# A two-layer graph attention kernel: the planner's lock is taken from the weights' dot products, and its leads are replaced

## The chip, the core and the metric

The kernel runs on one core of a Trainium2 chip. A core has five engines that run their own queues of instructions in order: TensorE (PE in the profile, with its weight loads as PEld), VectorE (DVE), ScalarE (ACT), GpSimd (POOL) and SyncE (SP, which here only issues DMAs). The metric is the device time of one execution in microseconds. The kernel before takes 3507.43 us, the median of three runs (3507.41 to 3511.81).

## The reference

For each of 32 graphs with 512 nodes and 512 features (fp32) and a 0/1 adjacency matrix, two residual layers are computed. Each normalises its input, applies a relu and adds a graph attention:

```
h = relu(layernorm(x));  x = x + GAT0(h, adj)      # one head, no weights matrix
h = relu(layernorm(x));  x = x + GAT1(adj, h)      # 4 heads of 256, elu, then 1 head of 512

GAT0: s_src = h @ w_src;  s_dst = h @ w_dst
      attn = softmax(mask(leaky_relu(s_src[i] + s_dst[j] + b)))   ;  out = attn @ h
GAT1: xl = h @ W1 (512 x 1024), per head asrc = <xl, a_src>, adst = <xl, a_dst>
      softmax(mask(leaky_relu(asrc[s] + adst[d]))) over s ;  out = attn^T @ xl + b1 ; elu
      the same again with W2 (1024 x 512), one head
```

`asrc` and `adst` are linear in `h`: `asrc = h @ (W1 a_src)`. The kernel uses this. It computes the dot products of the weights' rows with the attention vectors once, on VectorE, and stores them as two extra columns beside each block of weights, so that the projection itself yields the scores.

## The kernel before

**Tiles.** A graph's rows stand in 4 tiles of 128 nodes. x has two places in SBUF, the masks (`m`) five, large results (`big`: edge weights E, features, projections) nine, and PSUM eight banks (`acc`).

**Stages of a graph.** `load_x` (LX); `layer0_scores` (S0): statistics on ACT for graphs 0 and 1 (lines 686 and 691), the power -1/2 on POOL (711), the scaled features on ACT (723), two dots per tile on DVE for the scores (`dot`, line 508, called at 1024 to 1030), an add on POOL (1032), the adjacency's mask on DVE (988, 993) and its transposed copy by SP (958). Then the guard, an upper bound of each row's scores: a row of scores is spread over the partitions by TensorE (`spread`, 676), DVE takes masked maxima (838), POOL adds (845), DVE joins (856). `edge_weights`: per tile a subtraction on POOL (882), a maximum and add on DVE (887), an exponential on ACT (894). `layer0_out` (O0) multiplies E with the features on TensorE (906) and adds into x (924). `layer1_in` (I1): layernorm again, the features turned by copies on ACT (743, 759) and transposing DMAs of SP (750), then `x + b2` on POOL (1074) and a spill of x to DRAM (1082). `layer1_project` (P1) and `layer2_project` (P2) multiply with the weights by a seven-product scheme (Strassen's in Winograd's form; TensorE at 1216), for which POOL forms the sums S1 to S4 of the input's quarters (1098) and the weights have the combinations T1, T2, T3 and -T4. The heads follow (H0 to H3), then `layer2_out` (O2).

**Constants.** Once, at the start, `load_constants` fetches the weights; `scores_1` makes 32 dots over W1's rows (4 row blocks, 4 heads, source and target; 256 elements each), `scores_2` 32 dots over W2's rows and 8 small adds (605); `column_sums` sums W2's columns on TensorE (622) and corrects b2 (637); `sums` forms T1, T2, T3 and -T4 of each matrix, values and score columns apart, on DVE or POOL (657, 658). The score columns of a combination need all the dots of their matrix. P1's second product, S1 times T1, needs T1 with its columns.

**The planner.** The kernel first records all operations with their engines, costs, reads and writes, then `Plan.draft` writes each engine's order by list scheduling: at every step the engine that can start soonest takes its best ready operation, the one with the smallest rank. The rank is the TensorE work recorded ahead of it less 1000 times its lead (`run`), so a larger lead goes first. A lead's name is stage, engine and the number of the operation's kind in that stage: `first S0g:DVE2` is the guard's line 838 of graph 0, `first Clater:DVE3` the dots of W1, `first Clater:DVE4` the weights' sums, `first Clater:DVE5` and `DVE6` the dots of W2, `first Clater:PE8` the column sums, `second S0:DVE7` the feature dots of graph 1. The stages "first", "second" and "last" have leads of their own; the graphs between share theirs.

Operations with `lock=True` on DVE and on POOL exclude each other in the plan:

```
bufs, locks = ops[i][4], ops[i][6]
if locks and e in lock and lock["POOL" if e == "DVE" else "DVE"] > at:
    heapq.heappush(later[e], (lock["POOL" if e == "DVE" else "DVE"], rank[i], i))
    continue
```

If both engines can start at the same instant, the one that stands first in `("PE", "ACT", "DVE", "POOL", "SP")` is served. The lock lives in the plan alone. On the chip only the queues' order and the data's semaphores hold. The tile `junk`, into which all dots, guards and ACT's statistics write values that nobody reads, isn't in the planner's lists either, but the chip's semaphores do order its writers.

Of the kernel before, what the change touches and what calls it, by code (L numbers as in the profile page):

```python
# [43 lines left out]
class Plan:  # L44
# [8 lines left out]
        "first LXsoon:SP0": 67.5, "first Csoon:SP0": 22.3, "first C:SP0": 15.3, "first Csoon:DVE1": -520.9,  # L53
        "first Clater:DVE0": -150.2, "first Clater:SP1": 22.3, "first Clater:DVE2": -516.8, "first S0:ACT0": -617.3,
        "first S0:ACT1": -146.3, "first S0:DVE2": 659.4, "first S0:POOL3": 88.2, "first S0:POOL4": 350.9,
        "first S0:POOL5": -561.2, "first S0:ACT6": 1450.6, "first S0:DVE7": 1411.7, "first S0:POOL8": 870.8,
        "first S0M0:POOL0": 546.3, "first S0M0:DVE1": 311.3, "first S0M0:DVE2": 215.9, "first S0M0:SP3": -1427.8,
        "first S0g:POOL0": -1064.9, "first S0g:PE1": 1717.7, "first S0g:DVE2": 2207.5, "first S0g:POOL3": 846.3,
        "first S0g:DVE4": 3270.6, "first S0e:PE0": -477.2, "first S0e:ACT1": 639.1, "first S0e:POOL2": 1171.2,
        "first S0e:DVE3": 2003.2, "first S0e:ACT4": -114, "first Clater:DVE3": -15523.5, "first Clater:DVE4": -6168.4,  # L60
        "first O0:PE0": -531.4, "first O0:DVE1": -1568.2, "first O0:DVE2": -1088.3, "first Clater:DVE5": -144,
        "first Clater:DVE6": -139.3, "first Clater:DVE7": -897.5, "first Clater:PE8": -49490.4,
        "first Clater:DVE9": -882, "first Clater:DVE10": -993.2, "first Clater:DVE11": -2114.6,
        "first I1:ACT0": -1609.1, "first I1:ACT1": -981.7, "first I1:DVE2": 2894.1, "first I1:POOL3": 3384.7,
        "first I1:POOL4": 3602.7, "first I1:ACT5": -3080.8, "first I1:ACT6": -1207.6, "first I1:SP7": 2767.8,
        "first I1:ACT8": 845.2, "first I1:POOL9": -46.6, "first I1:SP10": -39.2, "second LX:SP0": 301.3,
        "second S0:ACT0": -634.4, "second S0:ACT1": -693.1, "second S0:DVE2": 700.7, "second S0:POOL3": 276.3,
        "second S0:POOL4": 1432.6, "second S0:POOL5": 675.4, "second S0:ACT6": 939.6, "second S0:DVE7": -886.2,
        "second S0:POOL8": 373.7, "second S0M0:POOL0": -592, "second S0M0:DVE1": 8.3, "second S0M0:DVE2": -1244.9,
        "second S0M0:SP3": -919, "second S0g:POOL0": 121.2, "second S0g:PE1": 813.7, "second S0g:DVE2": -737.4,  # L70
        "second S0g:POOL3": 325.2, "second S0g:DVE4": 922.4, "second S0e:PE0": -189.2, "second S0e:ACT1": 1520.1,
        "second S0e:POOL2": 943.7, "second S0e:DVE3": -3018.4, "second S0e:ACT4": -5889.6, "M1:POOL0": -333.9,
        "M1:DVE1": -1310.6, "M1:DVE2": -589.2, "M1:SP3": -1290.8, "P1:POOL0": -315.8, "P1:POOL1": 534, "P1:PE2": -554,
        "P1:ACT3": -366.6, "P1:DVE4": -307.5, "S10:ACT0": -625.6, "S10:PE1": -313.7, "S10:SP2": -162.3,
# [311 lines left out]
def kernel(  # L386
# [187 lines left out]
    def scores_1(att):  # L574
        for k in range(KD):
            for h in range(H):
                q, kk = QUARTER[k // (KD // 2)][h % 2], k % (KD // 2)
                for i in range(2):
                    op(
                        "DVE", on_dve(F + 125),  # L580
                        lambda w=w1_s[q][:, kk, h // 2, :], i=i, h=h: dot(
                            w[:, 2:], flat(att[0])[:, i * HF + h * F : i * HF + (h + 1) * F], w[:, i : i + 1]
                        ),
                        W["w1"]((q, kk)) + att[0](i), W["w1"]((q, kk, h // 2, i)), LATER, lock=True,
                    )

    @plan.part("C")
# [869 lines left out]
```

## Time and profile before

| | us |
|---|---|
| median of three runs | 3507.43 |
| profiled execution, device time | 3510.15 |
| its span, first to last instruction | 3508.4 |
| TensorE busy | 3408.4 |
| TensorE idle from 0 to its first instruction (26.55) | 26.5 |
| TensorE idle from 26 to 122 | 42.8 |
| TensorE idle from 122 to 300 | 13.4 |
| TensorE idle from 400 to 3300 | 8.5 |
| DVE busy from 26 to 122 | 82.4 |
| 64 dots of the weights, one (median) | 0.43 |

Times in the lines of the profile count from the start of the span. In a timeline's line stand the start, the duration, the engine, the line of the kernel, the operation, what it writes and reads, and in brackets the idle time of its engine just before, with what released it. An L508 is one dot; the read of its accumulator (0.08) that overlaps its end is a record of its own, so that dots follow each other every 0.47 us. The 512-element L508 with `ws_r` or `wd_r` are the features' dots of S0; those over `w`, `w_T` and `big` are the weights'.

### The profile page before, as it was taken

To read this page: it belongs to the slowest core of one execution; us is meant where nothing else is said; L and a number is where in the kernel's file an instruction comes from. 1 tells how busy PE (TensorE), PEld (TensorE's weight loads), DVE (VectorE), ACT (ScalarE), POOL (GpSimd) and SP (SyncE) were. 2 spreads that over 40 slices of the span, in tenths; PEclk is the share of its full clock that TensorE was granted. 3 is DMA by queue.
4 is the path that set the end of the run, shared out by engine and by line. 5 is a ranking of instruction groups with operands and counts; after the bars stand their busy time and mean duration, and the time that the engine had idled before them with its cause. 6 is when DMAs were issued, how large, how long until landed. Compare 5 with 4: busy or idle time off the path is not lost.

```text
span 3508.4 us, 49234 instructions
## 1 busy us (share of the span) xinstructions
PE 3408.4 (97%) x15678; PEld 2929.5 (83%) x15678; DVE 2640.2 (75%) x7294; ACT 2067.7 (59%) x3288; POOL 1756.7 (50%) x1929
## 2 busy tenths in 40 slices
PE   4799999999999999999999999999999999999999
PEld 3677888888888888888888888888888888888888
DVE  6875877777877777777777777777777777787674
ACT  3674665556665555665555665555755565755563
POOL 2454455554455554555454555454555454555442
PEclk8899999999999999999999999999999999999999
DMA  5444655555655555655555655555655555655632
GB/s 147 117 124 95 138 147 134 136 143 114 141 138 137 138 140 110 151 137 137 140 133 114 155 136 136 139 136 112 157 134 136 140 134 114 150 136 136 145 88 76
DMA packets 732125, 462.14 MB, mean 132 GB/s; under 512 B 553596, under 2 KB 592728, under 8 KB 731864
## 3 DMA queue, kind: packets, MB, share of 16 engines
q1 hardware_dynamic: 698072, 425.42, 47.6%
q0 software_dynamic: 33792, 33.56, 6.7%
q8 instruction: 124, 2.03, 0.2%
q14 instruction: 137, 1.12, 0.1%
HBM read 289.93 MB, written 68.27 MB: 102 GB/s over the span
## 4 chain that ended last, share of the span: by engine, by line
PE 93%; DVE 3%; DMA 2%; ACT 1%; issue 1%; POOL 1%; DVEq 0%; SPq 0%; POOLq 0%; ACTq 0%
PE acc L906 50%; PE acc L1216 42%; PE acc L790 1%; DVE junk L508 1%; DVE guard L856 1%; DMA big<-row 1%; DVE junk L838 1%; DMA m<-m 0%; DMA v<-row 0%; ACT big L894 0%; DVE big L887 0%; ACT junk L691 0%; ACT junk L686 0%; ACT big L759 0%; POOL big L882 0%
## 5 line engine op out<-in xcount | busy, mean ns | idle before, releaser
L906 PE MATMUL acc<-big,big 128*128 128x257 f32 (+1 forms) x8192 | 1942.4, 381 | 18.8 <-ACT big L894 14.6
L906 PEld LDWEIGHTS acc<-big,big 128*128 128x128 f32 x8192 | 1539.9, 190 | 270.4 <-ACT big L894 22.2
L882 POOL TENSOR_TENSOR big<-m,big 128x512 f32<-128x512 bf16 x768 | 883.6, 1169 | 265.6 <-DMA big<-lines 214.5
L894 ACT ACTIVATE big<-big,ac 128x512 f32<-128x512 f32 x768 | 545.7, 720 | 190.5 <-DVE big L887 187.1
L887 DVE SCALAR_TENSOR_TENSOR big<-acc,ac,big 128x512 f32<-128x512 f32 x768 | 566.9, 743 | 92.9 <-POOL big L882 85.3
L838 DVE CUSTOM_DVE_ANT_0 junk<-m,acc 128x512 bf16<-128x512 bf16 x768 | 520.8, 678 | 53.3 <-ACT acc L817 38.2
L1216 PE MATMUL acc<-w_T,sum 128*128 128x258 f32 (+1 forms) x2048 | 506.8, 381 | 17.3 <-POOL big L490 15.2
L1216 PE MATMUL acc<-w,big 128*128 128x258 f32 (+1 forms) x2048 | 517.4, 381 | 3.8 <-ACT big L759 3.5
L731 ACT COPY big<-acc 128x258 f32<-128x258 f32 (+1 forms) x376 | 139.9, 374 | 561.1 <-PE acc L1216 556.8
L1216 PEld LDWEIGHTS acc<-w_T,sum 128*128 128x128 f32 x2048 | 387.2, 190 | 73.9 <-POOL big L490 15.6
L1216 PEld LDWEIGHTS acc<-w,big 128*128 128x128 f32 x2048 | 386.3, 190 | 64.6 <-ACT big L759 4.3
L732 DVE COPY big<-acc 128x258 f32<-128x258 f32 (+1 forms) x392 | 166.1, 424 | 326.0 <-PE acc L1216 323.2
L1227 DVE TENSOR_TENSOR big<-acc,big 128x258 f32<-128x258 f32 (+1 forms) x576 | 241.2, 420 | 117.8 <-PE acc L1216 116.0
L1299 ACT ACTIVATE v<-acc,minus_one 128x256 f32<-128x256 f32 x512 | 228.4, 470 | 147.6 <-DVE acc L1292 83.7
L759 ACT COPY big<-v 128x1024 uint16<-128x1024 uint16 x256 | 295.9, 1157 | 22.0 <-DMA v<-row 21.8
L743 ACT COPY row<-v 128x1024 uint16<-128x1024 uint16 x256 | 265.7, 1040 | 13.1 <-DMA v<-row 10.9
L924 DVE SCALAR_TENSOR_TENSOR x<-acc,r,x 128x256 f32<-128x256 f32 x512 | 240.0, 480 | 39.1 <-PE acc L906 31.8
L1216 PE MATMUL acc<-w,sum 128*128 128x258 f32 (+1 forms) x1024 | 254.8, 382 | 0.0
L1216 PE MATMUL acc<-w_-T,big 128*128 128x258 f32 (+1 forms) x1024 | 252.8, 380 | 0.0
L845 POOL TENSOR_TENSOR guard<-ac,guard 128x4 f32<-128x4 f32 (+1 forms) x128 | 26.1, 204 | 444.2 <-DVE guard L838 427.0
L1292 DVE SCALAR_TENSOR_TENSOR acc<-acc,r,b_r 128x256 f32<-128x256 f32 x512 | 238.9, 485 | 2.9
L1303 DVE SCALAR_TENSOR_TENSOR v<-v,acc 128x256 f32<-128x256 f32 x512 | 204.8, 411 | 47.0 <-ACT v L1299 43.8
(89 smaller groups left out, 3412.2 us busy)
## 6 DMA issues: line engine op xcount, KB each, us to landing
big<-lines SPq DMA_DIRECT2D x378, 256.0 KB
row<-lines SPq DMA_DIRECT2D x189, 256.0 KB
x<-in_x_dram SPq DMA_DIRECT2D x32, 1024.0 KB
m<-in_adj_dram POOLq DMA_DIRECT2D x64, 512.0 KB, 5.8
spill<-x SPq DMA_DIRECT2D x32, 1024.0 KB
x<-spill SPq DMA_DIRECT2D x32, 1024.0 KB
out_dram<-x SPq DMA_DIRECT2D x30, 1024.0 KB
v<-row SPq DMA_TRANSPOSE x256
```

Source lines behind the costliest of these rows:

```text
L743: lambda: nc.scalar.copy(e.at.bitcast(U16).rearrange("p (b f) -> p b f", b=2), values_of().bitcast(U16).rearrange("p (f b) -> p b f", b=2)),
L759: nc.scalar.copy(out.bitcast(U16).rearrange("p k t (n b) -> p k t n b", b=2), values_of().bitcast(U16).rearrange("p (b t k n) -> p k t n b ...
L838: lambda t=t, j=j, a_row=a_row: nc.vector.tensor_tensor_reduce(by_blocks(junk), mask_row(mask_max, t), by_blocks(a_row.at), 1.0, LOWEST, A ...
L882: lambda t=t: nc.gpsimd.tensor_sub(by_blocks(E.at[:, t, :]), mask_row(mask, t), by_blocks(g_at())),
L887: lambda t=t: nc.vector.scalar_tensor_tensor(E.at[:, t, :], c_row.at, ac.at[:, 4 + j, t : t + 1], E.at[:, t, :], op0=ALU.max, op1=ALU.add),
L894: lambda t=t: nc.scalar.activation(E.at[:, t, :], E.at[:, t, :], AF.Exp, bias=ac.at[:, 2 * j, t : t + 1]),
L906: lambda s=s: nc.tensor.matmul(acc.at[:, :n], E.at[:, s, node_block(t)], of(s), start=(s == 0), stop=(s == T - 1)),
L924: lambda acc=acc, r=r, f=f, t=t: nc.vector.scalar_tensor_tensor(X.at[:, t, f], acc.at[:, :HD], r.at, X.at[:, t, f], op0=ALU.mult, op1=ALU. ...
L1216: lambda k=k: nc.tensor.matmul(acc.at[:, :width], at[a](k // 2)[:, k % 2, node_block(r)], weight_of(w, k, c), start=(begin and k == 0), st ...
L1227: op("DVE", on_dve(width), lambda: nc.vector.tensor_add(place(), acc.at[:, :width], place()), acc(0) + token, token)
L1292: lambda acc=acc, r=r: nc.vector.scalar_tensor_tensor(acc.at[:, :F], acc.at[:, :F], r.at, b1_r[:, h * F : (h + 1) * F], op0=ALU.mult, op1= ...
L1299: lambda i=i, v=v, acc=acc: nc.scalar.activation(v.at[:, i, :], acc.at[:, :F], AF.Exp, bias=minus_one), acc(0), v(i),
```

## The change

The three dots of `scores_1` and `scores_2` lose `lock=True`, and all leads are replaced. The leads of the first two graphs' stages differ by tens up to some 3500, most others by less than 500. Operations, tiles and costs stay as they are.

```diff
@@ LEADS, first two graphs (cut)
-        "first LXsoon:SP0": 67.5, "first Csoon:SP0": 22.3, "first C:SP0": 15.3, "first Csoon:DVE1": -520.9,
-        "first Clater:DVE0": -150.2, "first Clater:SP1": 22.3, "first Clater:DVE2": -516.8, "first S0:ACT0": -617.3,
-        "first S0g:POOL0": -1064.9, "first S0g:PE1": 1717.7, "first S0g:DVE2": 2207.5, "first S0g:POOL3": 846.3,
-        "first S0e:DVE3": 2003.2, "first S0e:ACT4": -114, "first Clater:DVE3": -15523.5, "first Clater:DVE4": -6168.4,
-        "first O0:PE0": -531.4, "first O0:DVE1": -1568.2, "first O0:DVE2": -1088.3, "first Clater:DVE5": -144,
-        "first Clater:DVE6": -139.3, "first Clater:DVE7": -897.5, "first Clater:PE8": -49490.4,
-        "second S0:POOL4": 1432.6, "second S0:POOL5": 675.4, "second S0:ACT6": 939.6, "second S0:DVE7": -886.2,
...
+        "first LXsoon:SP0": 272.7, "first Csoon:SP0": 251.2, "first C:SP0": 231.6, "first Csoon:DVE1": -455.8,
+        "first Clater:DVE0": -799.2, "first Clater:SP1": 250.8, "first Clater:DVE2": -1192, "first S0:ACT0": -3047.4,
+        "first S0g:POOL0": -1249.6, "first S0g:PE1": 641.8, "first S0g:DVE2": 2149.6, "first S0g:POOL3": 805.5,
+        "first S0e:DVE3": 3211.7, "first S0e:ACT4": 979.6, "first Clater:DVE3": -19068.8,
+        "first Clater:DVE4": -8215.1, "first O0:PE0": -585, "first O0:DVE1": -1560.3, "first O0:DVE2": -1183.5,
+        "first Clater:DVE5": -1405.4, "first Clater:DVE6": -685, "first Clater:DVE7": -1171.6,
+        "first Clater:PE8": -51476.4, "first Clater:DVE9": -1153, "first Clater:DVE10": -1719.3,
+        "second LX:SP0": 304.9, "second S0:ACT0": -3211.6, "second S0:ACT1": -3099.1, "second S0:DVE2": 923,
+        "second S0:DVE7": -149.4, "second S0:POOL8": 776.6, "second S0M0:POOL0": -519.7, "second S0M0:DVE1": 18.4,
...
@@ scores_1
                         lambda w=w1_s[q][:, kk, h // 2, :], i=i, h=h: dot(
                             w[:, 2:], flat(att[0])[:, i * HF + h * F : i * HF + (h + 1) * F], w[:, i : i + 1]
                         ),
-                        W["w1"]((q, kk)) + att[0](i), W["w1"]((q, kk, h // 2, i)), LATER, lock=True,
+                        W["w1"]((q, kk)) + att[0](i), W["w1"]((q, kk, h // 2, i)), LATER,
@@ scores_2
-                    W["w2"]((q, kk)) + att[1](i), W["w2"](("part", k)), LATER, lock=True,
+                    W["w2"]((q, kk)) + att[1](i), W["w2"](("part", k)), LATER,
...
-                    W["w2"]((r, kk)) + att[1](i), W["w2"]((q, kk, i)), LATER, lock=True,
+                    W["w2"]((r, kk)) + att[1](i), W["w2"]((q, kk, i)), LATER,
```

## The prediction

> **What bounds the kernel now.** The page comes first: shares of the span, then the slices.
>
> ```profile
> span 3508.4 us, 49234 instructions
> PE 3408.4 (97%) x15678; PEld 2929.5 (83%) x15678; DVE 2640.2 (75%) x7294; ACT 2067.7 (59%) x3288; POOL 1756.7 (50%) x1929
> PE   4799999999999999999999999999999999999999
> PEclk8899999999999999999999999999999999999999
> ```
>
> TensorE is the bound, and only the first slices are not full. The table by stretches says where its 100 idle us lie.
>
> ```profile
> 26.00:57.00 31.00, 13.68 (x43) 10.86 (x44) 29.25 (x107) 3.51 (x5) 5.92 (x9) 0.75 0.61 159
> 57.00:107.00 50.00, 39.56 (x159) 31.92 (x157) 38.42 (x100) 26.95 (x51) 20.30 (x21) 0.88 0.46 89
> 107.00:122.00 15.00, 0.00 (x0) 0.00 (x0) 14.69 (x39) 9.05 (x13) 13.66 (x17) 0.59 0.49 132
> 122.00:300.00 178.00, 164.58 (x708) 138.09 (x709) 128.88 (x354) 115.67 (x190) 81.67 (x88) 0.94 0.46 115
> 400.00:3300.00 2900.00, 2891.48 (x13402) 2492.46 (x13401) 2228.19 (x6173) 1739.17 (x2735) 1495.68 (x1642) 1.00 0.56 135
> ```
>
> (Columns: length, then PE, PEld, DVE, ACT and POOL busy with their instruction counts, granted clock, DMA share, GB/s.) From 400 to 3300 TensorE lacks 8.5 us in 2900: nothing is to be had there. Between 107 and 122 it does nothing at all, while DVE is busy 14.69 of 15. The timeline of that stretch shows why; the first two lines and the last are DVE's and TensorE's, the one between is POOL's.
>
> ```profile
> 119.17 1.49 DVE L508 SCALAR_TENSOR_TENSOR junk<-w,big 128x256 bf16<-128x256 f32 x1
> 121.87 0.17 DVE L657 TENSOR_TENSOR w_T<-w_T,w 128x8 f32<-128x8 f32 x1
> 109.50 1.56 POOL L1098 TENSOR_TENSOR sum<-big 128x512 f32<-128x512 f32 x1 [0.82 <-ACT big L759]
> 122.14 6.05 PE L1216 MATMUL acc<-w_T,sum 128*128 128x258 f32 x16 [15.23 <-POOL big L490]
> ```
>
> The product that waits is S1 times T1. S1 is there at 109.50 + 1.56 = 111.06. T1's score columns are there at 121.87 + 0.17 = 122.04, since they need every dot product of W1, and the last of the 32 starts at 121.17. The profile names POOL's memset (121.94), but the product doesn't read what that writes; I read the wait as one for T1. The next lines show the other place where the dots hold the start back, the guard of graph 0 at 44.83.
>
> ```profile
> 32.44 1.04 PE L676 MATMUL acc<-ident,ac 128*128 128x128 f32 x8
> 44.83 0.68 DVE L838 CUSTOM_DVE_ANT_0 junk<-m,acc 128x512 bf16<-128x512 bf16 x1
> ```
>
> Its row is spread over the partitions by 33.5, and its mask was finished at 14.8; for 11.3 us it only stands in DVE's queue, behind W2's dots.
>
> **Part 1: the lock goes from the 64 dots of W1 and W2.** No instruction is added or removed; what changes is the order that the planner writes. In the planner a locked operation of POOL can't start before the locked operation of DVE under way ends, and at that same instant DVE is served first and takes its next dot. So a row of dots keeps POOL's locked work out of the plan until DVE runs out or takes an unlocked one. What starves behind W2's dots (26.4 to 44) is POOL's small work on graph 0's scores, which the row transposes (L676) and so the guard wait for. Without the lock that work is planned during the dots; the guard (lead 2207.5 before, 2149.6 after) stands far above W2's dots (-144 and -139.3 before; -1405.4 and -685 after), so it comes first when ready: at 33.5 instead of 44.83, 11.3 us earlier. SP's transposes of the masks are a bound here: the first is issued at 32.77 and lasts 5.9, so E of graph 0 can't start before some 39, against 56.96 today. They keep their place behind the weights' loads, whose leads rise.
>
> The second effect is on W1's dots, the lowest on DVE before and after (-15523.5, -19068.8). They fill gaps, and in the plan no longer only those in which POOL rests. From 26 to 122 DVE is idle 96 - 82.36 = 13.64 us, of which 11.6 lie between 57 and 107. With 32 dots of 0.43 + 0.04 us that is nearly all of W1's 15 us.
>
> What it is worth: S1 times T1 can start 122.14 - 111.2 = 10.9 us earlier as soon as T1 is no later than S1, which takes 10.9 of the 13.64. If the guard's 11.3 us also bring S1 forward, DVE without a gap would give 122.04 - 13.64 = 108.4 and a gain of 13.7. If the idle time is not the sort that a dot can fill (DVE waits at its head for TensorE or ACT, and the order is fixed), the gain is 0. I take 10.9, since one wait of 3.66 us at 65.1 and many under 1.4 stand in a stretch where dots are ready since 32.
>
> **What the chip takes back.** Whether dots and POOL exclude each other is in the trace already.
>
> ```profile
> 29.54 2.35 POOL L658 TENSOR_TENSOR w_T<-w,w_T 128x1020 f32<-128x1020 f32 x1 [1.27 <-DMA w<-in_L_gnn_W_dram]
> 29.66 2.51 DVE L508 SCALAR_TENSOR_TENSOR junk<-w_T,big 128x257 bf16<-128x257 f32 x1
> 76.58 3.03 DVE L508 SCALAR_TENSOR_TENSOR junk<-w,big 128x256 bf16<-128x256 f32 x1 [0.40 <-ACT junk L691]
> ```
>
> A dot of 0.43 us takes 2.51 when it starts 0.12 after a sum of POOL's, and ends 0.3 after that sum. Six dots are so stretched; the four between 111 and 121 (1.49, 1.37, 1.34, 1.49) lose 1.0 each. So the plan now leaves out something that is there. The Trainium skill says the same and speaks against the change: in "SBUF — State Buffer", section "Who interferes with whom", a DVE instruction with two SBUF inputs contends with a GpSimd instruction that reads SBUF, and the second of them fully blocks. By that page the dots would have to stay excluded, and every dot planned beside POOL would be a loss for DVE of the rest of POOL's instruction.
>
> The price goes by the rows: POOL reads SBUF in 20 long instructions between 56 and 121 (8 of L882, 4 of L1098, 8 of L1074), of which five already stretch a dot. At most some 14 more could, at 1.0 us, 14 us on DVE; at least none, because the dots' new places are also where POOL idles (from 64.9 to 75.1 it works 0.4 us). Fewer than today would be a gain of up to 8.7 us, the sum of the six excesses. I take 3 more, 3.0 us, of which the 13.64 - 10.9 = 2.7 us left of DVE's idle time cover nearly all: 0.3.
>
> **Part 2: the leads.** For the first two graphs hundreds to thousands of units move. The one that I can follow: graph 1's feature dots rise from -886.2 to -149.4, above W2's dots, so eight dots of 0.73 us (5.9 us) move ahead of W2's. Behind them are W2's column sums on TensorE, whose 44.21 start was waited for by nothing but b2's correction, and through it POOL's L1074, the spill on SP (101.22) and the load of graph 2 (106.19). If that load comes later than its place allows, graph 2's statistics (114) are late next; the cover is that they feed work first used after 300. So zero, up to 6 us if the cover is gone. The other leads of these stages move too (graph 1's statistics on ACT from -634.4 to -3211.6, behind graph 0's as before; L887 from 2003.2 to 3211.7, now above the guard it follows anyway); among steps that are ready together I find no other turn. The other leads change by tens to hundreds; from 400 to 3300 only 8.5 us of idle exist to win, and 2 us could as well be lost. Zero, with 3 to either side.
>
> **What is kept later.** Behind 122 TensorE is idle another 13.4 us up to 300, in waits of 3.4 (192.69), 3.6 (239.23) and 2.2 (279.55) for the heads' edge weights. Graph 1's projection starts at 147.9 and its last input copy ends at 135.8, so 11 us earlier is just covered (12.1). The heads' POOL work from 163.41 to 174.4 has TensorE at 174.92 without a wait; moved forward, it depends on row DMAs whose latency does not shrink. I charge 0.6.
>
> Sum: 10.9 - 0.3 - 0.6 = 10.0 us. Against the profiled execution's own 3510.15 (span 3508.4 and 1.75 around it) that is 3500.1; that execution lies 2.7 above the median of 3507.43, so the median to expect is 3497.4. The three runs spread by 4.4; about 0.2%, 7 us, is what can be told from no change.
>
> **Rivals.**
> *Slower: dots blocked by POOL.* For it: the six stretched dots. It decides where the stretches added exceed the DVE idle time filled. With 14 more at 1.0 and a guard that hardly moves (3 us filled), T1 comes 11 us later: 3518. Against it: POOL rests for most of 32 to 75, where the dots are to go.
> *Given back through the junk tile.* Dots and ACT's statistics write the same junk tile, which the planner's lists don't hold; DVE waited 6.6 + 1.0 us for ACT there and ACT 4.0 + 3.8 for DVE. Eight more such waits at the mean of 7.6/10 = 0.76 cost 6.1: 3503.5, within 0.2%.
> *More: the whole start moves.* With the guard 11.3 earlier, DVE's idle time filled (13.6) and six stretches gone (8.7), T1 comes at 99.7 and the start is some 22 us shorter: 3485. Against it: feature turning by DMA and ACT (101.86 to 109.4) follows the output of graph 0 and doesn't shrink.
> *Nothing.* If the order of the first 122 us stays as it is, 3507.
>
> **How the numbers follow.** The forecast (gain 7 to 15) 0.44; the whole start 0.12; given back 0.18; nothing 0.08; blocked 0.18. Faster is 0.44 + 0.12 = 0.56, same 0.18 + 0.08 = 0.26, slower 0.18. For 8 in 10 the range reaches from a little past the whole start, 3482, to part of the blocked case, 3515; the forecast's own is 3492 to 3501.
>
> **What would show it.** In the changed profile the guard L838 of graph 0 starts before 36; TensorE's first L906 before 55 instead of 62.04; the last dot of W1 ends before 112; the gap ahead of the first S1 times T1 falls from 15.2 to 5 or less; dots over 1 us number about nine; 400 to 3300 stays as it is. I am wrong if L838 still follows W2's dots, if more than 14 dots are stretched, or if TensorE's idle time between 122 and 400 grows by what the first 122 us gave.

## The result and the profile after

The changed kernel takes 3607.49 us (median of five runs, 3603.54 to 3611.53), beside 3511.32 for the kernel before on the same chip: a ratio of 1.0277, 95% interval 1.0265 to 1.0289. It is 2.8% slower, and far outside the predicted range of 3482 to 3515. The page of the kernel after, its span and its busy times:

```profile
span 3609.4 us, 49171 instructions
PE 3443.8 (95%) x15678; PEld 2952.1 (82%) x15678; DVE 2713.7 (75%) x7248; ACT 2069.2 (57%) x3327; POOL 1779.5 (49%) x1936
```

The span grew by 101 us. TensorE's own instructions take 35.4 us more than before (3443.8 against 3408.4) for the same 15678 matmuls, so about a third of the loss is a slower clock and the rest is idle time. The 40 slices show neither: TensorE stays at 9 in all but the first two, as before. The table by stretches, kernel after (columns as in the prediction):

```profile
107.00:122.00 15.00, 4.18 (x8) 2.35 (x8) 8.11 (x17) 10.71 (x22) 5.24 (x7) 0.55 1.04 205
122.00:300.00 178.00, 160.35 (x705) 133.28 (x706) 128.54 (x359) 122.04 (x201) 92.67 (x103) 0.95 0.53 130
400.00:1400.00 1000.00, 974.13 (x4455) 837.54 (x4454) 767.57 (x2042) 584.34 (x930) 504.12 (x549) 0.98 0.53 131
```

The start is not where the time went. Between 107 and 122 TensorE now works 4.18 us instead of 0, and by 400 us it has issued 1361 matmuls, before 1348; at 0.2155 us each (the middle of a later kernel: 999.60 us for 4638) the 13 more are 2.8 us. In the middle, which the prediction held to be untouched, TensorE is idle 25.87 us in the 1000 shown (3.1 before) and its granted clock is 0.98 (1.00 before). Per graph the period went from 105.44 us (603.55 to 708.99, one TensorE instruction of line 790 to the same one of the next graph) to 109.87 (620.85 to 730.72). The list of TensorE's waits names the place; first the kernel before from 400 to 3300, then the kernel after from 400 to 3700 (columns: total us, times, the longest):

```profile
PE acc L790 <- DVE guard L856: 6.8, 27, 0.5
```

```profile
PE acc L790 <- DVE v L1303: 76.2, 24, 3.2
```

A graph has four guards, one of layer 0, two of the heads of layer 1 and one of layer 2. All are joined on DVE by line 856, and their rows are turned on TensorE by line 790. The two rows above are not of the same guard.

Before, TensorE waited 0.25 us in 27 graphs for the join of layer 2. Single instructions of POOL held that join: it took 0.80 in most graphs, and 1.06 at most between 400 and 3300. One of them, in three lines of that timeline:

```profile
602.21 1.26 POOL L1098 TENSOR_TENSOR big<-big 128x512 f32<-128x512 f32 x1
...
602.44 1.05 DVE L856 SCALAR_TENSOR_TENSOR guard<-guard,guard 128x4 f32<-128x4 f32 x1
...
603.55 0.27 PE L790 MATMUL acc<-ident,guard 128*4 128x128 f32 x1 [0.48 <-DVE guard L856]
```

The join ends at 603.49, with POOL's sum (603.47). In the kernel after, this join takes 0.15 and no L790 waits for it.

After, TensorE waits 3.18 us in 24 graphs, and for another guard, that of layer 0 of the next graph. In the kernel before, its join took 0.15 in every graph, some 4 us behind the load of a mask (L948, `load_adj`), and in most graphs its L790 came 0.92 us after the join, without a wait:

```profile
616.98 0.85 POOL L948 DMA_DIRECT2D m<-in_adj_dram  x1 [0.30 <-POOL big L882]
...
621.28 0.15 DVE L856 SCALAR_TENSOR_TENSOR guard<-guard,guard 128x4 f32<-128x4 f32 x1
...
622.35 0.27 PE L790 MATMUL acc<-ident,guard 128*4 128x128 f32 x1
```

The wait after is put down to L1303, which is only the last of a queue, as the timeline of the kernel after around 615 us shows:

```profile
614.95 0.20 POOL L845 TENSOR_TENSOR guard<-ac,guard 128x4 f32<-128x4 f32 x1 [7.98 <-DVE guard L838]
...
615.19 0.47 DVE L1292 SCALAR_TENSOR_TENSOR acc<-acc,r,b_r 128x256 f32<-128x256 f32 x1
...
615.43 0.86 POOL L948 DMA_DIRECT2D m<-in_adj_dram  x1 [0.28 <-issue]
...
615.57 4.17 DVE L856 SCALAR_TENSOR_TENSOR guard<-guard,guard 128x4 f32<-128x4 f32 x1
...
616.31 4.64 POOL L882 TENSOR_TENSOR big<-m,big 128x512 f32<-128x512 bf16 x4
...
620.39 0.40 DVE L1303 SCALAR_TENSOR_TENSOR v<-v,acc 128x256 f32<-128x256 f32 x1
...
620.85 0.37 PE L790 MATMUL acc<-ident,guard 128*4 128x128 f32 x1 [3.18 <-DVE v L1303]
```

The join is an instruction of 128x4 elements with two inputs in SBUF. It now starts 0.14 us after POOL has begun to issue the load and takes 4.17 us instead of 0.15, until 619.74. That is about when the third of the four subtractions behind the load ends (616.31 + 3 x 1.16 = 619.79; the subtractions are those of layer 2's edge weights). On DVE everything else stands behind it: L1227, L1292, L1303; then TensorE's L790.

With the wait of 3.18 us the clock falls as well; stretches of the kernel after around it:

```profile
621.00:624.00 3.00, 3.00 (x9) 2.40 (x9) 2.25 (x6) 2.81 (x5) 0.00 (x0) 0.52 0.47 129
624.00:627.00 3.00, 3.00 (x15) 2.63 (x14) 2.45 (x7) 2.08 (x4) 0.00 (x0) 1.00 0.72 165
```

For the 3 us from 621 on the granted clock is 0.52, which loses 3.0 x 0.48 = 1.44 us. So one hold costs an estimated 3.18 + 1.44 = 4.6 us, and 24 like it 111 us. The 35.4 us more of TensorE's busy time, over 24, are 1.48 each, which agrees. The Trainium skill, "TensorE: Matmul & The Clock Gate", Part 1, section "What's actually happening", gives an idle window of about 3.4 us after which the clock is halved; here a little less, 3.18 us, was followed by it.

Of the 28 graphs between 400 and 3500 us, the join is held in 24. In two it begins 0.25 or 0.15 before the load (loads at 401.08 and 836.86) and takes 0.16 and 0.15. In the two others it begins 0.13 after it, as here in the timeline of the kernel after:

```profile
1711.10 0.86 POOL L948 DMA_DIRECT2D m<-in_adj_dram  x1 [0.29 <-issue]
...
1711.23 0.15 DVE L856 SCALAR_TENSOR_TENSOR guard<-guard,guard 128x4 f32<-128x4 f32 x1
```

0.13 us behind the load the join is free, at 0.14 it is held for 4.2 us. That is the clue on which the experiments are built.

### The profile page after: what moved, and what is told of

Same layout as the page of the kernel before. It is cut to its first block, busy times and chain, and to the rows that moved or that the text cites. A ratio compares the mean times of both kernels' runs of the same rounds, so it can differ in the third digit from the quotient of the medians.

```text
span 3609.4 us, 49171 instructions
## 1 busy us (share of the span) xinstructions
PE 3443.8 (95%) x15678; PEld 2952.1 (82%) x15678; DVE 2713.7 (75%) x7248; ACT 2069.2 (57%) x3327; POOL 1779.5 (49%) x1936
## 4 chain that ended last, share of the span: by engine, by line
PE 91%; DVE 3%; issue 1%; ACT 0%; ACTq 0%; DVEq 0%
PE acc L906 47%; PE acc L1216 43%; DVE guard L856 1%; PE acc L790 1%; DVE acc L1292 1%; DVE v L1303 0%; DVE big L1227 0%; DVE junk L838 0%; DVE r L1289 0%; DVE big L887 0%; ACT big L894 0%; ACT v L1299 0%; DVE m L988 0%; DVE x L924 0%; PE acc L676 0%
## 5 line engine op out<-in xcount | busy, mean ns | idle before, releaser
L906 PE MATMUL acc<-big,big 128*128 128x257 f32 (+1 forms) x8192 | 1948.2, 380 | 16.5 <-ACT big L894 12.5
L906 PEld LDWEIGHTS acc<-big,big 128*128 128x128 f32 x8192 | 1535.3, 190 | 263.6 <-ACT big L894 18.6
L882 POOL TENSOR_TENSOR big<-m,big 128x512 f32<-128x512 bf16 x768 | 883.3, 1169 | 134.5 <-DMA big<-lines 98.9
L887 DVE SCALAR_TENSOR_TENSOR big<-acc,ac,big 128x512 f32<-128x512 f32 x768 | 558.8, 742 | 119.9 <-ACT acc L817 63.8
L838 DVE CUSTOM_DVE_ANT_0 junk<-m,acc 128x512 bf16<-128x512 bf16 x768 | 520.2, 677 | 68.9 <-ACT acc L817 61.1
L1216 PEld LDWEIGHTS acc<-w,big 128*128 128x128 f32 x2048 | 402.5, 197 | 76.3 <-ACT big L759 11.0
L731 ACT COPY big<-acc 128x258 f32<-128x258 f32 (+1 forms) x436 | 161.7, 373 | 501.0 <-PE acc L1216 496.8
L1299 ACT ACTIVATE v<-acc,minus_one 128x256 f32<-128x256 f32 x512 | 236.7, 471 | 246.6 <-DVE acc L1292 191.2
L845 POOL TENSOR_TENSOR guard<-ac,guard 128x4 f32<-128x4 f32 (+1 forms) x128 | 26.3, 205 | 650.2 <-DVE guard L838 586.5
L1227 DVE TENSOR_TENSOR big<-acc,big 128x258 f32<-128x258 f32 (+1 forms) x576 | 240.7, 420 | 137.6 <-PE acc L1216 136.6
L732 DVE COPY big<-acc 128x258 f32<-128x258 f32 (+1 forms) x332 | 139.8, 421 | 194.6 <-PE acc L1216 194.4
L1216 PE MATMUL acc<-w_T,big 128*128 128x258 f32 (+1 forms) x1024 | 283.9, 410 | 0.0
L1292 DVE SCALAR_TENSOR_TENSOR acc<-acc,r,b_r 128x256 f32<-128x256 f32 x512 | 244.1, 483 | 1.8
```

Source lines behind the costliest of these rows:

```text
L838: lambda t=t, j=j, a_row=a_row: nc.vector.tensor_tensor_reduce(by_blocks(junk), mask_row(mask_max, t), by_blocks(a_row.at), 1.0, LOWEST, A ...
L882: lambda t=t: nc.gpsimd.tensor_sub(by_blocks(E.at[:, t, :]), mask_row(mask, t), by_blocks(g_at())),
L887: lambda t=t: nc.vector.scalar_tensor_tensor(E.at[:, t, :], c_row.at, ac.at[:, 4 + j, t : t + 1], E.at[:, t, :], op0=ALU.max, op1=ALU.add),
L906: lambda s=s: nc.tensor.matmul(acc.at[:, :n], E.at[:, s, node_block(t)], of(s), start=(s == 0), stop=(s == T - 1)),
L1216: lambda k=k: nc.tensor.matmul(acc.at[:, :width], at[a](k // 2)[:, k % 2, node_block(r)], weight_of(w, k, c), start=(begin and k == 0), st ...
L1227: op("DVE", on_dve(width), lambda: nc.vector.tensor_add(place(), acc.at[:, :width], place()), acc(0) + token, token)
```

## The experiments

Two theories stood at the outset. **The hold**: the loss is the join of layer 0 that meets the load and the subtractions behind it, an accident of the order that the new leads give the shared stages of the graphs. **The lock**: the loss comes from the dots no longer excluding POOL, or from the first graph's new leads, and the middle suffers from what the start hands on. In all kernels below the line numbers of the shown lines are shifted by what the edit adds above them (up to 13).

**Only the lock and the first graph's leads.** The dots have no lock; the leads whose names begin with "first" are the new ones, all others the old.

```diff
-        "second LX:SP0": 304.9, ... , "M1:POOL0": -308.5, ... , "last M1:POOL0": -47.9, ...
+        "second LX:SP0": 301.3, ... , "M1:POOL0": -333.9, ... , "last M1:POOL0": 3.8, ...
```

> The change's unlocked dots and its leads for graph 0 and the constants (the names that begin with first), all other leads as before. The changed kernel loses 3.18 us of TensorE in 24 of the graphs from 400 us on, so if the loss is made by the leads of the middle graphs, this kernel keeps the old period of 105.4 us per graph and differs from before by the start alone. Start theory from the changed profile (by 400 us it had issued 1363 matmuls against 1350, 13 x 0.215 = 2.8 us ahead): 0 to 5 us faster, ratio 0.9985 to 1.000. The forecast's theory of the start (10 us): ratio 0.997. If the dots' collisions with GpSimd cost the start (six stretched dots of 2.44 us and S1 times T1 at 128.3 instead of 122.1): 6 us slower, ratio 1.0017. If taking the lock away is what makes the loss in every graph: period near 109.9, ratio 1.027.

Measured: 3516.89 us, before 3511.78, ratio 1.0013 (1.0004 to 1.0021). The period of most graphs in the middle is 105.44 as before, and between 400 and 3300 no join is held longer than 1.06 us. So neither the lock nor the first graph's leads make the 96 us by themselves. What this half of the change does by itself is a loss at the edge of what can be told. The first L906 starts at 70.00 (62.04 before), S1 times T1 at 127.93 (122.14 before), and 15 dots are stretched by 21.13 us in all.

**A pause ahead of the load.** One memset of a tile that nobody reads stands on POOL between the guard's add (L845) and the load.

```diff
+            if best.engine[i] == "POOL":
+                if lead.endswith("M1:POOL0") and last.endswith("S0g:POOL4"):
+                    self.pause()       # nc.gpsimd.memset(unread, 0.0), 128x96
+                last = lead
```

> The changed kernel with one more GpSimd instruction, a memset of 128x96 fp32 to a tile that nobody reads, ahead of those adjacency loads that follow a guard's add on GpSimd at once (28 graphs). Nothing else moves. In the changed profile the guard's join L856 on DVE starts 0.14 us after the load and then takes 4.17 us (24 graphs), or 0.13 after and takes 0.15 (2 graphs). Theory, port held by GpSimd from about 0.14 us after the load's start through the subtractions that follow: the memset (0.1 to 0.2 us) puts the load behind the join's start, the join takes 0.15, TensorE's 3.18 us go and the time falls by 24 x 4.4 = 106 us to about 3502, ratio to before 0.998. Rival, the order on TensorE or the queue of DVE ahead of it makes the wait: the time stays at 3607, ratio 1.027. Rival, the memset itself is joined to the block: the join is stretched in all 28 graphs, 3625.

Measured: 3606.04 us, ratio 1.0267 (1.0253 to 1.0281). The pause was no pause, as the timeline of this kernel shows:

```profile
720.26 0.18 POOL L470 MEMSET unread<- 128x96 f32 x1
720.60 0.86 POOL L955 DMA_DIRECT2D m<-in_adj_dram  x1 [0.17 <-issue]
720.75 4.17 DVE L863 SCALAR_TENSOR_TENSOR guard<-guard,guard 128x4 f32<-128x4 f32 x1
```

The load starts 0.48 after the add with the memset as without it: the 0.18 us vanish in the 0.28 us that POOL needs between an instruction and a DMA issue. So the run decides nothing between the theories. It does sharpen the clue: 21 joins are held here instead of 24, and some at the same 0.14 us take 0.15 (behind the loads at 615.56 and 1383.08). The two outcomes lie within the trace's last digit of each other.

**Four memsets ahead of the load.** The same edit with four of them.

> As the run with one memset, but four memsets of 128x96 between the guard's add and the adjacency load. With one, the load still started 0.48 us after the add, since 0.28 us of that gap are issue time which the memset filled; four (about 0.17 us apart) should put it at about 1.0 us after the add, and the join, which starts 0.6 us after the add, ahead of the load by 0.4. Theory (the join is caught because it starts while the load's issue takes the port, and the subtractions behind it keep it out): the join takes 0.15 us in all 28 graphs, the waits of 3.18 us go, and the time is that of before plus or minus the start: 3500 to 3520, ratio 0.997 to 1.0025. Rival, order on TensorE or DVE: 3600, ratio 1.026.

Measured: 3511.08 us, before 3510.65, ratio 1.0003 (0.9994 to 1.0012). The timeline:

```profile
612.18 0.15 DVE L863 SCALAR_TENSOR_TENSOR guard<-guard,guard 128x4 f32<-128x4 f32 x1
...
612.91 0.86 POOL L955 DMA_DIRECT2D m<-in_adj_dram  x1 [0.33 <-issue]
```

The load now comes 0.73 after the join, which takes 0.15 in all graphs, and the loss is gone. Nothing was changed on DVE; four instructions that compute nothing made the kernel 2.7% faster.

**The load behind the subtractions.** The load moves on POOL behind the four L882, where the kernel before had it.

```diff
...
+            if self.ops[b][5].endswith("M1:POOL0") and self.ops[a][5].endswith("S0g:POOL4"):
+                behind = pool[pool.index(b) + 4]
+                order.remove(b)
+                order.insert(order.index(behind) + 1, b)
```

> The changed kernel with the same adjacency loads issued behind the four subtractions L882 that follow them instead of ahead. The join now meets the subtractions alone. If the load's issue is what holds DVE and a subtraction only makes it wait for its own end: the join takes up to 1.2 us, TensorE does not wait, about 3502, ratio 0.998. If a run of subtractions keeps DVE out, as the end of the 4.17 us at the end of the third of them suggests: the join takes 3.4 to 4.6 us, TensorE waits 2.4 to 3.6 us in every graph, 3585 to 3625, ratio 1.021 to 1.032. If the join starts before the first subtraction takes hold: 0.15 us and 3502.

Measured: 3531.37 us, before 3511.78, ratio 1.0057 (1.0041 to 1.0072). Timeline (POOL, then DVE) and one of TensorE's waits from 400 on:

```profile
616.73 4.65 POOL L888 TENSOR_TENSOR big<-m,big 128x512 f32<-128x512 bf16 x4
617.20 0.71 DVE L862 SCALAR_TENSOR_TENSOR guard<-guard,guard 128x4 f32<-128x4 f32 x1
```

```profile
PE acc L912 <- ACT big L900: 27.1, 25, 3.7
```

Without a load in front, the same four subtractions hold the join for the rest of the one under way: 617.20 + 0.71 = 617.91, and the first subtraction ends near 617.9. So the order of load and subtractions matters, not the subtractions alone. TensorE doesn't wait for this join. What is left of the loss here is another wait, for the edge weights E: 27.1 us, of the 38.8 by which this kernel lies above the next one.

**A gap between the load and the subtractions.** The four memsets stand behind the load; the load keeps its moment.

```diff
+                if last.endswith("S0g:POOL4") and lead.endswith("M1:POOL0"):
+                    lead = "load behind an add"
+                elif last == "load behind an add":
+                    self.pause()       # four memsets
+                last = lead
```

> The same four memsets, but between the load and the first subtraction L882. The join still starts 0.14 us after the load. If the join is held by the load until its end and then loses to each subtraction in turn only because they follow without a gap: it ends in the gap, takes 0.7 to 0.9 us, and the time is about 3510 to 3530, ratio 1.000 to 1.005. If whatever the load starts lasts some 4 us by itself (the descriptors being written or read, until the load lands 5 to 6 us later): the join still takes about 4.2 us and the time stays near 3607, ratio 1.027.

Measured: 3492.57 us, before 3510.65, ratio 0.9947 (0.9934 to 0.9961). Neither theory had that. Timeline:

```profile
610.52 0.86 POOL L957 DMA_DIRECT2D m<-in_adj_dram  x1 [0.27 <-issue]
...
610.67 0.15 DVE L865 SCALAR_TENSOR_TENSOR guard<-guard,guard 128x4 f32<-128x4 f32 x1
...
612.25 4.66 POOL L891 TENSOR_TENSOR big<-m,big 128x512 f32<-128x512 bf16 x4
```

The join starts 0.15 after the load, the place at which it was held, and takes 0.15, in all graphs. So the load by itself holds nothing, and my first form of the theory (the load's issue keeps the join out) falls. The subtractions hold, but at a moment when the trace doesn't show them running yet.

**One memset, and two more runs to read it.** To tell the length of the gap from what stands next to the load, the same edit with one memset.

> The changed kernel with one memset (0.18 us, it only writes) between load and first subtraction, where four gave a join of 0.15 us and 3492.6. If what holds DVE is the instruction that stands next behind the load and reads SBUF (its port being taken while the load is still issued), one memset is as good as four: join 0.15, 3485 to 3500, ratio 0.993 to 0.997. If a gap of about the join's 0.7 us or more between load and subtraction is needed: the join is stretched again, 3600, ratio 1.025.

Measured: 3495.98 us, before 3511.41, ratio 0.9956 (0.9942 to 0.9969). Timeline:

```profile
609.80 0.86 POOL L957 DMA_DIRECT2D m<-in_adj_dram  x1 [0.27 <-issue]
609.94 0.15 DVE L865 SCALAR_TENSOR_TENSOR guard<-guard,guard 128x4 f32<-128x4 f32 x1
...
610.80 1.19 POOL L891 TENSOR_TENSOR big<-m,big 128x512 f32<-128x512 bf16 x1
```

The join is free 0.14 after the load. I read this as a matter of kind: an instruction that only writes, next behind the load, and the hold is gone. But the memset also moved the first subtraction by 0.12 us, so that the join starts 0.86 ahead of it; in the kernel after it was held at 0.74 (616.31 - 615.57) and free at 0.75 (1711.98 - 1711.23). Distance explains it as well, and two runs tell the two apart. In the first a tiny subtraction that reads SBUF takes the memset's place; in the second the memset stays and DVE does three tiny memsets ahead of the join, which makes it later.

```diff
-    plan.pause = lambda: nc.gpsimd.memset(unread, 0.0)
+    plan.pause = lambda: nc.gpsimd.tensor_sub(unread[:, :4], still[:, :4], still[:, 4:8])      # the first
+    plan.delay = lambda: [nc.vector.memset(still, 0.0) for _ in range(3)]                      # the second:
+            if lead.endswith("S0g:DVE5"):
+                self.delay()
```

> In place of the one memset, a subtraction of 128x4 elements (two inputs in SBUF, some 0.2 us) stands between the load and the first L882, so that the first large subtraction starts about 1.00 us after the load, as with the memset. What the kernel computes is unchanged. If the KIND of instruction next behind the load decides (one that reads SBUF holds, one that only writes doesn't), the join that starts 0.14 after the load is held again, for 3 to 4.2 us, in most of the 28 graphs, TensorE's L790 waits 50 to 80 us in all, and the time is 3570 to 3610 us. If the DISTANCE decides (the join is free when it starts 0.75 us or more ahead of the first large subtraction: 0.74 was held and 0.75 free in the kernel after, 0.86 free with the memset), the join takes 0.15 and the time is 3491 to 3499.

> One memset stands between the load and the first L882, and on DVE three memsets of 128x24 elements of an unread tile go ahead of the join, so that it starts some 0.2 to 0.4 us later: 0.35 to 0.55 after the load and only 0.45 to 0.65 ahead of the first large subtraction, nearer than the 0.74 at which it was held in the kernel after. What the kernel computes is unchanged. If the KIND of instruction next behind the load decides, the join still takes 0.15 and the time is 3493 to 3502. If the DISTANCE to the first large subtraction decides, the join is held for some 3.5 to 4.2 us in most graphs and the time is 3570 to 3610.

Measured: 3493.88 us (ratio 0.9950, 0.9936 to 0.9965) and 3618.91 us (1.0305, 1.0288 to 1.0322), both beside 3511.07 before. The timelines, first the tiny subtraction, then the later join:

```profile
612.30 0.86 POOL L959 DMA_DIRECT2D m<-in_adj_dram  x1 [0.27 <-issue]
612.45 0.19 DVE L867 SCALAR_TENSOR_TENSOR guard<-guard,guard 128x4 f32<-128x4 f32 x1
...
613.19 0.22 POOL L474 TENSOR_TENSOR unread<-still 128x4 f32<-128x4 f32 x1
...
613.35 4.66 POOL L893 TENSOR_TENSOR big<-m,big 128x512 f32<-128x512 bf16 x4
```

```profile
616.13 0.86 POOL L961 DMA_DIRECT2D m<-in_adj_dram  x1 [0.28 <-issue]
...
616.66 3.88 DVE L869 SCALAR_TENSOR_TENSOR guard<-guard,guard 128x4 f32<-128x4 f32 x1
...
617.11 1.19 POOL L895 TENSOR_TENSOR big<-m,big 128x512 f32<-128x512 bf16 x1
```

Kind falls in both. With a reading instruction next to the load the join is free of the large subtractions; with a memset next to the load, but only 0.45 ahead of the first subtraction, it is held in 27 graphs, and the loss is back and somewhat larger (the forecast for it ended at 3610). In the one graph of that kernel where the join starts 0.84 ahead (401.19 against 402.03), it takes 0.13, so it isn't DVE's memsets that hold it. What counts is whether the join starts more or less than about 0.75 us ahead of the record of the first large subtraction. It is as if the subtractions behind a load took hold 0.74 us before their record begins: 615.57 in the kernel after, 617.11 - 0.74 = 616.37 in the last run. From there to the join's end it is 4.17 us in both (619.74; 616.66 + 3.88 = 620.54). The tiny subtraction can be read in the same way: its record starts 0.74 after the join (613.19 - 612.45), and the join takes 0.19 instead of 0.15, in nearly all graphs; at 0.13 after the load it takes 0.15 in that kernel as well.

The Trainium skill, "SBUF — State Buffer", section "Who interferes with whom", says that a DVE instruction with two SBUF inputs contends with a GpSimd instruction that reads SBUF, and that the order of issue decides who blocks. By the records the join was first (615.57 against 616.31) and should have been free; the section agrees with the runs only if a subtraction behind a load is taken to begin 0.74 ahead of its record. The join then waits past three of them, and not for one; the measured 4.17 us stand.

**Two instructions of DVE change places.** POOL is as in the kernel after. On DVE the join goes ahead of the L1292 that stood just before it.

```diff
...
+            lead = self.ops[a][5].split(":")
+            if self.ops[b][5].endswith("S0g:DVE5") and lead[0][-2:] in ("H0", "H1", "H2", "H3") and lead[1] == "DVE2":
+                order.remove(a)
+                order.insert(order.index(b) + 1, a)
```

> The changed kernel with GpSimd's order untouched. On DVE the guard's join L856 changes places with the head's scaling L1292 (0.38 us) just ahead of it, so that it starts some 0.2 us before the adjacency load instead of 0.14 after. In the changed profile the one join that started 0.15 before its load took 0.15 us. Theory (only the moment counts at which the join asks for the port): all 28 joins take 0.15, the waits of 3.18 us go, and the time is that of the run with memsets behind the load, 3485 to 3500, ratio 0.993 to 0.997. Rival (the order load, then subtractions, holds DVE whatever the moment): 3607, ratio 1.027.

Measured: 3494.33 us, before 3511.41, ratio 0.9948 (0.9933 to 0.9963). The timeline:

```profile
613.75 0.16 DVE L862 SCALAR_TENSOR_TENSOR guard<-guard,guard 128x4 f32<-128x4 f32 x1
...
613.99 0.86 POOL L954 DMA_DIRECT2D m<-in_adj_dram  x1 [0.28 <-issue]
```

The join starts 0.24 before the load in place of 0.14 after it. Nothing is added or left out on any engine, and 1.0277 - 0.9948 = 3.3% of the time come back, 115 us. With this the cause of the loss is shown: the moment of the join against load and subtractions. The hold goes in three independent ways (load later, subtractions later, join earlier), and each time the loss goes with it. Made later again, the join brings it back. What GpSimd does between a load and the record of the next subtraction isn't shown.

It also shows what the change was worth without the accident: some 15 to 19 us in the four kernels that keep the load's moment (0.9947, 0.9948, 0.9950 and 0.9956), though none in the one with four memsets ahead of it (1.0003). The middle of the kernel with four memsets behind the load, first its row by stretches, then TensorE's only wait from 400 on:

```profile
400.00:1400.00 1000.00, 999.60 (x4638) 862.60 (x4637) 763.71 (x2110) 596.99 (x956) 537.26 (x611) 1.00 0.55 135
```

```profile
PE acc L915 <- ACT big L903: 3.3, 6, 1.0
```

TensorE is idle 0.4 us in 1000 there (3.1 before) and does 4638 matmuls (4621 before). From 400 to 3400 this adds up to 57 matmuls more, an estimated 57 x 0.2155 = 12 us; the rest, some 6 us, is the start and the end. So the middle did have something to give: about all of the 8.5 us of idle time that the prediction put out of reach, if not more (a few matmul records can be missing from a trace). Most of it has a name: 6.8 of the 8.5 us were the waits for layer 2's join, which the new shared leads free. It takes 0.15 here, and still 0.80 in the first kernel above, which has the old ones.

**The weights' sums on DVE.** In the start, POOL makes T1 to T4 of both matrices (L658) beside the dots, and each of the large sums holds a dot. Here the sums all go to DVE, whatever engine the plan chose.

```diff
-            emit[engines.index(best.engine[i])]()
+            by = 0 if lead == "first Clater:DVE4" else engines.index(best.engine[i])
+            emit[by]()
```

This was laid on three of the kernels above: the first one (lock and first graph's leads), the one with four memsets ahead of the load, and the one with four behind it.

> The kernel with unlocked dots and new leads for the first stage alone, which was 0.13% slower than before, with the weights' sums that its plan gives to GpSimd (L658, 5 between 42 and 52 us, each stretching a dot from 0.43 to about 2.4 us, and two at 98) done on DVE at the same place in the order (1.2 us each). If the collisions of dots and sums cost the start: GpSimd is free at 42 for the edge weights of graph 0 (L882 at 58.5 there), TensorE's first L906 comes at about 58 instead of 70, and the time falls by 5 to 12 us below that kernel, to a ratio of 0.998 to 1.000 against before. If the first real product doesn't set the end of the start (the turned input and S1 at 127.9 do): no gain, ratio 1.001.

> The changed kernel with the four memsets ahead of the load and with all weights' sums on DVE: both causes taken away at once. If the two are independent, the gain of the sums on DVE comes on top of that of the memsets: 5 to 12 us below the run with memsets alone, about 3495 to 3505, ratio 0.995 to 0.998. If the start doesn't matter for the end, the same time as with the memsets alone.

> The changed kernel with four memsets behind the load and with the weights' sums on DVE. The memsets alone gave 3492.6 (ratio 0.9947); the sums on DVE gave 6 and 8 us in two kernels. If they add up here too: 3483 to 3488, ratio 0.992 to 0.9935. If the start doesn't reach the end here: 3492.

Measured: 3507.03 (ratio 0.9995, 0.9986 to 1.0004), 3503.10 (0.9979, 0.9970 to 0.9988) and 3487.05 us (0.9931, 0.9918 to 0.9943). Against the kernels without this edit that is 0.18, 0.24 and 0.16%, 6 to 8 us each time (in the last pair the two intervals overlap): it adds to the rest. The stretched dots go from 15 (21.13 us) to 8 (7.28 us) in the first pair, and S1 times T1 from 127.93 to 119.99. So POOL's sums beside the dots cost the start 6 us or more. Two things go with them, the stretching of the dots and POOL's own time ahead of graph 0's first subtraction (42.04 here), and these runs don't separate the two. The last of the three beats both kernels, by 0.7% the one before; its page:

```profile
span 3487.5 us, 49275 instructions
...
PE 3401.3 (98%) x15678; PEld 2923.5 (84%) x15678; DVE 2610.0 (75%) x7258; ACT 2066.1 (59%) x3327; POOL 1793.7 (51%) x2038
```

## Why the prediction was wrong

The failed step is the last of part 2: "The other leads change by tens to hundreds; from 400 to 3300 only 8.5 us of idle exist to win, and 2 us could as well be lost. Zero, with 3 to either side." Measured, this term is a loss of some 93 us: 1.0277 with the new shared leads against 1.0013 with the old ones, everything else alike (the second and the last graph's leads went along). By the estimates above the held join makes 111 us of loss, and the rest of the new order a gain of about 12. I bounded the term by the idle time that could be won; the 2 or 3 us for what could be lost had no row behind them.

No wait in the kernel before pointed at this join: layer 0's had 0.92 us to spare, and the one that TensorE waited for was layer 2's. But the hold itself was there, in a line that the prediction shows, the dot at 76.58 that took 3.03 us. What POOL did beside it in the kernel before:

```profile
76.18 0.82 POOL L948 DMA_DIRECT2D m<-in_adj_dram  x1
...
77.03 3.60 POOL L882 TENSOR_TENSOR big<-m,big 128x512 f32<-128x512 bf16 x3
```

The dot starts 0.40 behind a load and 0.45 ahead of the first subtraction's record, and ends at 79.61, past the second subtraction (78.15 + 1.17 = 79.32). I counted it as one of six stretched dots and didn't ask what held it before any subtraction ran. An excess of 2.6 us, less the 0.92 to spare, on a join in each of 28 graphs would have been an estimate of 47 us.

Four shared leads in the diff bear on the place. The guard's add and the load rise (`S0g:POOL4` 267.6 to 320.2, `M1:POOL0` -333.9 to -308.5), the join and the subtractions of layer 2 fall (`S0g:DVE5` 22.7 to -67.1, `P2e:POOL2` -663.4 to -712.8). I didn't read them for the order that they make. Which of them is to blame wasn't separated: the leads were only exchanged in groups. Two readings of the prediction were wrong besides, without weight in its sum. The wait of 3.6 us at 239.23 is for a guard's join (L856), not for edge weights, and the mask's transpose at 32.77 lasts 4.83 us (5.9 is the one at 95.21).

The rival *slower* had the right kind of cause, a DVE instruction with two SBUF inputs held by POOL, at the wrong place and in the wrong instruction: dots in the start, worth 11 us, instead of a join once per graph.

The start, point by point:

- *Guard L838 of graph 0 before 36.* Right: 28.14. But the guard is more than its maxima.
- *First L906 before 55 instead of 62.04.* Wrong: 72.89. The timeline of the kernel after, lines of DVE, POOL and TensorE:

```profile
42.43 0.16 DVE L856 SCALAR_TENSOR_TENSOR guard<-guard,guard 128x4 f32<-128x4 f32 x1
...
48.44 2.33 POOL L658 TENSOR_TENSOR w_-T<-w,w_T 128x1020 f32<-128x1020 f32 x1
48.45 2.60 DVE L508 SCALAR_TENSOR_TENSOR junk<-w,big 128x257 bf16<-128x257 f32 x1
...
58.25 2.45 POOL L882 TENSOR_TENSOR big<-m,big 128x512 f32<-128x512 bf16 x2
...
72.89 11.31 PE L906 MATMUL acc<-big,big 128*128 128x257 f32 x40 [5.57 <-ACT big L894]
...
128.30 5.75 PE L1216 MATMUL acc<-w_T,sum 128*128 128x258 f32 x16 [8.84 <-POOL sum L1098]
```

  The join of graph 0 starts at 42.43, although its add is done at 31.3: eight dots of graph 1's features and W2's first dots now stand ahead of it on DVE. Then POOL, which the plan lets work beside the dots, makes five of the weights' sums (43.23 to 53.25) and waits 4.73 us for W2's scores with a sixth (57.98) before the first subtraction at 58.25. I had named this overtaking (graph 1's feature dots, 5.9 us) and looked for its price only behind W2's dots, not at the join.
- *Last dot of W1 before 112.* Right: it starts at 106.11 and ends at 107.47. The dots did fill DVE's idle time.
- *Gap ahead of S1 times T1 from 15.2 to 5 or less.* Half right: 8.84, and it is now POOL's sum S1 that releases it (126.96 + 1.29 = 128.25), not T1. The wait for T1 is gone, as forecast, but S1, which I left at 111, came 17 us later with all of graph 0, and TensorE waits another 9.33 us ahead of the product before it (114.76). The gain of 10.9 was taken against a fixed S1.
- *About nine stretched dots, 0.3 us.* The count was 13 and their excess 20.05 us, 11.4 more than before (8.65): the term of 3.0 us was mis-sized nearly fourfold. W2's dots beside the sums cost 2.0 each rather than the 1.0 that I took from those between 111 and 121.
- *400 to 3300 stays as it is.* Wrong, the step above.
- *TensorE's idle time from 122 to 400 doesn't take back the start.* Right: 17.7 us after, 16.4 before. The start as a whole gains 2.8 us by 400.

What stays open. That a subtraction behind a load holds DVE 0.74 us ahead of its record is what the joins of all these kernels fit; what GpSimd does in that time, and why the join is let in only after the third record's end, the traces don't show. And the kernel with four memsets ahead of the load is some 18 us slower than that with four behind it, of which TensorE's waits for E show 8.8 - 3.3 = 5.5; the rest wasn't found.

## What to carry to other kernels

Price a change of order in a loop by what it could lose, times the number of turns: a join with 0.92 us to spare was held for 4.17, and 4.6 us per graph became 111. One line of the kernel can serve several stages: the L856 that TensorE waited for before and the L856 that was held after are different joins, and only what stands around them in the timeline tells them apart. A longer wait is put down to the last instruction of a queue, so look in the timeline for the one whose duration is wrong for its size (128x4 in 4.17 us) before asking what it waits for. A planner's exclusion of two engines is only as good as its list of instructions and its durations: here the join and the subtractions are both locked, but the load between them isn't, and the plan counts 2.2 us for its issue where the trace shows 0.86. No run changed that figure.

## What the runs showed of the hardware

- A VectorE instruction with two SBUF inputs that takes 0.15 us was held for 3.9 to 4.2 us by four GpSimd subtractions behind a DMA issue. It was held when it started up to about 0.75 us ahead of the first one's record (0.75 at 3355.74 in the kernel after), and free from about there on (0.74 at 615.70 in the kernel with one memset ahead of the load): between the two lies the trace's last digit.
- In the kernel before, a dot that started 0.45 us ahead of the first of three subtractions behind an issue was held past the second, 3.03 us in place of 0.43.
- Without the issue in front, the same subtractions held it until the end of the one under way (0.71).
- A memset of 0.18 us ahead of the issue didn't move it: it fitted into the 0.28 us that lie between a GpSimd instruction and a DMA issue.
- A wait of TensorE of 3.18 us, until 620.85, was followed by about 3 us at a granted clock of 0.52 (621 to 624).
